# Elements 0, 1 and 31 as lists of single steps, with sums over all keys and half-size output products at the end

## The chip, the cores and the metric

The kernel runs on one core of one Trainium2 chip. The metric is device time in microseconds (us), the median of several runs. The engines that matter here are TensorE (PE: matrix products and transposes through the array), VectorE (DVE), ScalarE (ACT) and SyncE (SP, which issues nearly all transfers). Each engine works through its own queue in program order.

## The reference

32 batch elements, each with 512 nodes of 512 features (`x`) and a 512x512 adjacency (`adj`), go through two layers, all in float32. Cut to what is computed:

```python
# layer 0, H = 8 heads of 64
q, k, v = heads(x @ Wq.T + bq), heads(x @ Wk.T + bk), heads(x @ Wv.T + bv)
logits = einsum('bhqd,bhkd->bhqk', q, k) / sqrt(64)
logits = logits + log(clip(adj, 1e-8, None))[:, None]
attn = softmax(logits)                       # over the keys
out = einsum('bhqk,bhkd->bhqd', attn, v).reshape(b, n, d) @ Wo.T + bo
x = layer_norm(x + out, gamma, beta)
# layer 1, on the same adjacency
f = x @ fc_w.T + fc_b
q, k = f @ q_w.T + q_b, f @ k_w.T + k_b      # one number a node
m = leaky(q + k.T + (1 - adj) * -1e9)        # slope 0.01
y = softmax(m) @ f + x
```

## The kernel before

One element after the other. The work of neighbouring elements overlaps: while the attention of element b runs, layer 0's output product and norm and the weights of layer 1 of element b-1 (`last`) are done, and the last products of element b-2 (`gone`). Tiles hold 128 partitions; a 512x512 matrix is four tiles of 128x512. The engines' queues are filled in the order in which the Python program issues, so that order is the schedule.

Layer 0 of an element. The query, key and value products and the output product are computed by seven half-size products instead of eight (sums of quarters on VectorE, `halves` at L221, 64 columns of weights at a time, 256 wide). Heads go in four pairs. For each pair, scores are computed with the keys on the partitions (L946), ScalarE takes the exponent (L953, L955), VectorE multiplies by the clipped adjacency `cT`, turned beforehand (L963, L981: `factor`), and the value product uses the result `at` (L1049, `value_steps`). The softmax is divided out only after the value product: the sums over the keys become reciprocals `R`, spread over partitions by a round trip through DRAM (`divided`, L1114 and around), and multiply the pair's output `oT`.

These sums are taken in one of three ways. For elements 2 to 30 VectorE adds the four key tiles (L1004), turns the sum in blocks (L1008) and sums rows (L1015): "folded". For elements 0 and 1 and the first two pairs of 31, VectorE adds the four tiles to `as` (L973, L976), and `divide` multiplies that by ones on TensorE (four products a call, L1071); a ScalarE copy (L1077) and a trip through DRAM follow. For pairs 2 and 3 of 31, `divide_here` multiplies `as` by ones (L1153) and forms the reciprocal in place.

Layer 1 of an element: row dots `k` and `q` (L409), `k` spread to all partitions through DRAM (`store_k`, `load_k`: `kst`, `kld`), the mask from the adjacency (`le0`, `le1` load it), the exponent and row sums `r` (`weight_steps`), then z = weights times x with seven products (`z_steps`, sums at L1228 to L1234; the weights turned by VectorE at L636), or with whole products (`z_units`, L335) and TensorE transposes (L328), and the output product of z with `fc` (`out_steps` by seven products, or `out_units` by whole ones, L549), which VectorE adds with the residual (`yb`).

Order. Elements 2 to 30 run by two lists of single steps, `FIRST` and `SECOND`, through `perform`. In them `S0` to `S7` are score products, `f..` factors, `V..` value products, `m` products by sevens of queries and keys (`q`, `Q`), values (`v`), the output product (`w`), z (`z`) and out (`o`), `d` the differences of the next element's x, `c` the turns of the next adjacency, `la` its 16 transfers, `dv0`, `dv2` the `divided` steps, `s..` and `t..` the sums over keys. Elements 0, 1 and 31 run by functions: `slot(b, p)`, one head pair a call, with coarser units; `joining_slot(31)` and `last_slot`, `last_layer1` for the end. Before element 0 come the first transposes of x by TensorE (L656), the first queries and keys by whole products (L335) and the folding of the vectors into the weights (`fold_units`: `bias`, `offset`, `spread`).

Elements 29 and 30 differ from the others: their softmax rows are not normalised, and the factor `r` enters when the output is added (L557). Element 29's z is by sevens, element 30's by whole products with TensorE transposes; out is by whole products for both, in halves for the last. Element 31's layer 1 is by sevens throughout.

A range check (`find_range`: `over_elements`, `turn`, `over_partitions`) reduces flags on the sums to one number, `flag`; the engines load it at the end (L2009) and branch (L2011) to a general version of the kernel that the given data never need. Its last parts stand among the last products.

Of the kernel before, what the change touches and what calls it, by code (L numbers as in the profile page):

```python
# [9 lines left out]
FP = mybir.dt.float32  # L10
I32 = mybir.dt.int32
AF = mybir.ActivationFunctionType
ALU = mybir.AluOpType
# [17 lines left out]
def kernel(  # L31
# [151 lines left out]
    def combine_units(S, a11, a12, a21, a22):  # L183

        def three():
            nc.vector.tensor_add(S[:, 0], a21, a22)
            nc.vector.tensor_sub(S[:, 1], S[:, 0], a11)
            nc.vector.tensor_sub(S[:, 2], a12, S[:, 1])
        return [three, lambda: nc.vector.tensor_sub(a21, a11, a21)]
# [45 lines left out]
    def fold_units(psum, scratch):  # L235
# [15 lines left out]
        def row_times(col, w, name):  # L251

            ps = psum.tile([P, D], FP, tag="m", name=f"ps_{name}")
            for c in range(DC):
                nc.tensor.matmul(
                    ps, col[:, c : c + 1].to_broadcast([P, P]), w[:, c, :],
                    start=(c == 0), stop=(c == DC - 1),
                )
            return ps
# [6 lines left out]
        def bias():  # L266
            nc.vector.tensor_add(K["bo"], K["bo"], row_times(bvc, K["wo"], "bvwo"))
            nc.vector.tensor_sub(K["bo"][:, H:], K["bo"][:, H:], K["bo"][:, :H])
            for w, col, _, _, _, _ in vectors:
                for c in range(DC):  # L270
                    nc.vector.scalar_tensor_tensor(
                        junk, K["fc"][:, c, :], 1.0, w, ALU.mult, ALU.mult,
                        accum_out=col[:, c : c + 1],
                    )

        def offset():
            nc.vector.tensor_add(K["cc"], K["cc"], row_times(bc, K["fc"], "bfc"))
            nc.vector.tensor_add(K["cc"], K["cc"], fcb)
            nc.vector.tensor_sub(K["cc"][:, H:], K["cc"][:, H:], K["cc"][:, :H])
            for w, col, part, dg, _, b0 in vectors:  # L280
                nc.vector.tensor_mul(part, col, bc)
                nc.vector.scalar_tensor_tensor(
                    junk, fcb, 1.0, w, ALU.mult, ALU.mult, accum_out=extra[:, 1:2]
                )
                nc.vector.tensor_add(b0, b0, extra[:, 1:2])
                nc.vector.tensor_mul(col, col, gc)
                for c in range(DC):
                    nc.vector.tensor_scalar_mul(dg[:, ts(c, P)], ident, col[:, c : c + 1])
            for c in range(DC):
                nc.vector.tensor_scalar_mul(  # L290
                    K["fc"][:, c, :], K["fc"][:, c, :], gc[:, c : c + 1]
                )

        def spread(psum_parts):
            def copy(vector):
                _, _, _, dg, name, _ = vector
                ps = psum.tile([P, D], FP, tag="m", name=f"ps_{name}")
                nc.tensor.matmul(ps, ones, dg, start=True, stop=True)
                nc.vector.tensor_copy(K[name], ps)

            for vector in vectors:
                copy(vector)
            ps = psum_parts.tile([P, D], FP, tag="po", name="ps_parts")
            for i, (_, _, part, _, _, _) in enumerate(vectors):
                nc.tensor.matmul(ps[:, ts(i, DC)], ones, part, start=True, stop=True)
            for i, (_, _, _, _, _, b0) in enumerate(vectors):
                nc.vector.tensor_reduce(extra[:, 0:1], ps[:, ts(i, DC)], AX.X, ALU.add)  # L307
                nc.vector.tensor_add(b0, b0, extra[:, 0:1])

        return [bias, offset, spread]  # L310
# [163 lines left out]
    def weight_steps(s, small, name):  # L474
# [7 lines left out]
        def logit(c):  # L482
            qk = s["w"][:, (2, 3, 0)[c % 3], :]
# [83 lines left out]
    def fast(ctx):  # L567
# [9 lines left out]
        folded = {(b, p) for b in range(2, B - 1) for p in (0, 2)}  # L577
# [41 lines left out]
        def load_e(b, half=None):  # L619
# [3 lines left out]
            if b == B - 1:  # L623
                s["e"] = cT
            elif b == B - 2:
                s["e"] = K["qk_s"].rearrange("p a b f -> p (a b) f")[:, :NC, :]
            else:
                s["e"] = L1
# [19 lines left out]
        def first_xT():  # L648
# [3 lines left out]
            pt = [ps_m.tile([P, N], FP, tag="m", name=f"pt_x_{i}") for i in range(3)]  # L652
            pt.append(ps_o.tile([P, N], FP, tag="po", name="pt_x_3"))
            for c in range(NC):
                for i in range(DC):
                    nc.tensor.transpose(pt[i][:, ts(c, P)], s["n"][:, c, ts(i, P)], ident)  # L656
            for i in range(DC):
                (nc.scalar.copy, nc.vector.tensor_copy)[i % 2](s["xT"][:, i, :], pt[i])

# [12 lines left out]

        def first_qk(wq, wk):
            qk_tiles(0, 0)
            s = S[0]
            return qk_units(s, wq, wk, 0, s["qT", 0], s["kT", 0], ps_m, 0)
# [20 lines left out]

        def differences(b):
            run(difference_steps(b))
# [54 lines left out]
        def seven_qk(b, p):  # L754
            s = qk_steps(b, p)
            return [
                lambda names=names: run(s[n] for n in names.split())
                for names in ("m1 m5 cb ck2", "m6 m2 cq2 cq1", "m4 m3 ck1", "m7", "aq2 ak2 ak1")
            ]

# [38 lines left out]
        def seven_v(b):  # L799
            s = v_steps(b, long_banks(b))  # L800
            return [
                lambda names=names: run(s[n] for n in names.split())
                for names in ("m1 m5 cb c22", "m6 m2 c12 c11", "m7 m3 a22 a12", "m4 c21")
            ]

# [34 lines left out]
        def wo_steps(b, banks, apart=False):  # L840
# [9 lines left out]
            if apart:  # L850
                data["21"] = [third[:, c, :] for c in range(KH)]
# [16 lines left out]
            steps = row_steps(data, sub, K["wo_s"], K["wo"], lambda n: ps[n], add, apart)  # L868
            return steps | {"seed": seed}

        def seven_wo(b, banks, apart=False):
            s = wo_steps(b, banks, apart)

            def unit(names):
                return lambda: run(s[n] for n in names.split())
            adds = [[s[n] for n in names.split()] for names in (
                "s11 a11", "s12 a01 a00", "b11 b01", "a10 b10" if apart else "a10")]
            return [s["seed"]] + [
                unit(names) for names in ("m1 m5 cb", "m2 m6", "m3 m7", "m4")
            ], adds  # L880
# [77 lines left out]
        def factors(b, p, half):  # L958

            s = S[b]  # L960
            for kc in (2 * half, 2 * half + 1):
                at = s["at", p, kc]
                nc.vector.scalar_tensor_tensor(  # L963
                    at, cT[:, kc, :].unsqueeze(1).to_broadcast([P, 2, N]), ADJ_MIN, at,
                    ALU.max, ALU.mult,
                )

        def sums(b, p, half):

            s = S[b]  # L970
            if half == 0:
                s["as", p] = act.tile([P, 2, N], FP, tag="at", name=f"as_{b}_{p}", bufs=8)
                nc.vector.tensor_add(s["as", p], s["at", p, 0], s["at", p, 1])  # L973
            else:
                for kc in (2, 3):
                    nc.vector.tensor_add(s["as", p], s["as", p], s["at", p, kc])  # L976

# [7 lines left out]

        def both(b, p):
            run(values(b, p))

        def sums_in_place(b, p):

            s = S[b]
            to = s["as", p] = s["at", p, 0]
            return [
                lambda kc=kc: nc.vector.tensor_add(to, to, s["at", p, kc]) for kc in range(1, NC)
            ]
# [65 lines left out]
        def values(b, p):  # L1061
            v = value_steps(b, p)
            return [v["a"], lambda: (v["b"](), v["e"]())]

        def divide(b, p):


            s = S[b]
            ps = lone[0]
            for h in range(4):  # L1070
                nc.tensor.matmul(  # L1071
                    ps[h * BL : (h + 1) * BL, :], ones[:, :BL], s["as", p + h // 2][:, h % 2, :],
                    start=True, stop=True,
                )
            s["R", p] = act.tile([P, 2, N], FP, tag="R", name=f"R_{b}_{p}")
            r = s["R", p][:, 0, :]
            nc.scalar.copy(r, ps)  # L1077
            m = 4 * N // P
            d0 = dram.tile([4, N], FP, tag="d0", name=f"d0_{b}_{p}")
            nc.sync.dma_start(out=d0, in_=r.rearrange("(h r) n -> h r n", r=BL)[:, 0, :])  # L1080
            c = small.tile([P, 2, m], FP, tag="c", name=f"c_{b}_{p}", bufs=2)
            nc.sync.dma_start(out=c[:, 0, :], in_=d0.rearrange("h (a m) -> (h a) m", m=m))
            s["c", p] = c
# [974 lines left out]
```

## Time and profile before

| | us |
|---|---|
| median of 3 runs | 3292.02 (3288.52 to 3293.7) |
| profiled execution | 3290.96 |
| its span | 3289.1 |
| TensorE, VectorE, ScalarE busy | 3265.4, 3075.6, 1461.7 |
| granted TensorE clock | 0.998 |

The span runs from the first to the last record of the profiled execution. The times of the engines' rows overlap a little with the next row's, since operations are pipelined: from start to start a 64-column, 256-wide product unit takes 0.2156 us (two records), a 128-column, 512-wide one 0.86, a 64-column, 512-wide one 0.43. In the profile L12 means line 12 of the kernel, an arrow names what is written and read, and a wait says what the waiting engine waited for and how long in all, how often, and the longest.

### The profile page before, as it was taken

Reading aid. Unit: us, or ns where it says so; the run is one execution under the profiler, and the core shown is the slowest. Engines: PE = TensorE matmul, PEld = TensorE weight load, DVE = VectorE, ACT = ScalarE, POOL = GpSimd, SP = SyncE. Lnnn points to the kernel's source line nnn. Section 1 sums busy time; section 2 is a strip of 40 time slices with the busy share of each in tenths; the row PEclk is TensorE's granted clock in tenths of the full one; section 3 lists DMA queues with packets and bytes.
Section 4 is the critical chain, followed back from the end, with each engine's and each line's share of the span. In section 5 each row is a group of like instructions: output and inputs, shape, how many; then the busy total and the mean of one; then the engine's idle time right before and its main releaser. Section 6 shows DMA issues by size and latency. Waiting matters only on the chain.

```text
span 3289.1 us, 63772 instructions
## 1 busy us (share of the span) xinstructions
PE 3265.4 (99%) x25450; PEld 1885.3 (57%) x25450; DVE 3075.6 (94%) x5319; ACT 1461.7 (44%) x2733; POOL 1.0 (0%) x10
## 2 busy tenths in 40 slices
PE   9999999999999999999999999999999999999999
PEld 4555555555555555555556555555555555555545
DVE  7889999999999999999999999999999999999998
ACT  3435434444444354344444443543445444445432
POOL 0000000000000000000000000000000000000000
PEclk9999999999999999999999999999999999999999
DMA  5243433443433434334434334343343333442421
GB/s 129 42 79 70 89 75 65 85 90 70 86 69 71 95 70 88 71 65 89 88 71 84 68 73 95 68 89 72 61 95 84 75 82 66 76 96 64 95 70 43
DMA packets 914598, 256.14 MB, mean 78 GB/s; under 512 B 839908, under 2 KB 842212, under 8 KB 914296
## 3 DMA queue, kind: packets, MB, share of 16 engines
q1 hardware_dynamic: 914296, 252.01, 38.0%
q8 instruction: 202, 3.31, 0.5%
q14 instruction: 100, 0.82, 0.1%
HBM read 183.88 MB, written 36.55 MB: 67 GB/s over the span
## 4 chain that ended last, share of the span: by engine, by line
PE 97%; DVE 2%; ACT 1%; DMA 0%; issue 0%; SPq 0%; DVEq 0%; ACTq 0%
PE f L221 23%; PE mx L221 15%; PE my L221 15%; PE mz L221 15%; PE po L1049 13%; PE sc L946 7%; PE my L946 2%; PE mx L946 2%; PE mz L946 2%; DVE at L963 0%; PE my L335 0%; PE mz L549 0%; ACT n L399 0%; DMA n<-in_x_dram 0%; DVE R L409 0%
## 5 line engine op out<-in xcount | busy, mean ns | idle before, releaser
L981 DVE SCALAR_TENSOR_TENSOR at<-cT,at 128x1024 f32<-128x1024 f32 x468 | 557.1, 1211 | 1.8 <-ACT at L953 1.8
L1049 PE MATMUL po<-at,v 128*64 128x512 f32 x2048 | 486.5, 596 | 1.3 <-DVE fold_more L307 0.9
L726 ACT ACTIVATE qT<-f,bq 128x256 f32<-128x256 f32 x254 | 115.3, 470 | 805.0 <-PE f L221 805.0
L1004 DVE TENSOR_TENSOR at<-at,at 128x1024 f32<-128x1024 f32 x348 | 418.2, 1209 | 0.0
L955 ACT ACTIVATE at<-sc 128x1024 f32<-128x1024 f32 x270 | 272.7, 1072 | 48.1 <-PE sc L946 48.1
L1049 PEld LDWEIGHTS po<-at,v 128*64 128x64 f32 x2048 | 140.4, 137 | 230.2 <-issue 138.9
L221 PE MATMUL f<-xT,wq 128*64 128x256 f32 x2032 | 262.5, 379 | 0.0
L946 PE MATMUL sc<-qT,kT 64*128 64x512 f32 x1080 | 256.9, 592 | 0.3 <-ACT at L955 0.3
L221 PE MATMUL f<-T,qk_s 128*64 128x256 f32 x2032 | 256.4, 379 | 0.1
L221 PEld LDWEIGHTS f<-xT,wq 128*64 128x64 f32 x2032 | 146.3, 137 | 100.3 <-issue 36.0
L221 PEld LDWEIGHTS f<-T,qk_s 128*64 128x64 f32 x2032 | 146.1, 137 | 85.9 <-issue 16.6
L946 PEld LDWEIGHTS sc<-qT,kT 64*128 64x128 f32 x1080 | 103.7, 187 | 131.1 <-issue 87.2
L726 ACT ACTIVATE kT<-f,bk 128x256 f32<-128x256 f32 x254 | 120.0, 472 | 120.7 <-PE f L221 119.2
L1008 DVE STREAM_TRANSPOSE at<-at 128x1024 f32<-128x1024 f32 x116 | 142.3, 1227 | 1.0
L1015 DVE TENSOR_REDUCE ks<-at 128x32 f32<-128x1024 f32 x116 | 139.6, 1204 | 1.0
L221 PE MATMUL f<-xT,qk_s 128*64 128x256 f32 x1016 | 131.2, 379 | 0.0
L221 PE MATMUL f<-T,wk 128*64 128x256 f32 x1016 | 131.2, 379 | 0.0
L221 PE MATMUL f<-xT,wk 128*64 128x256 f32 x1016 | 131.2, 379 | 0.0
L946 PE MATMUL mz<-qT,kT 64*128 64x512 f32 x252 | 130.5, 598 | 0.0
L946 PE MATMUL my<-qT,kT 64*128 64x512 f32 x246 | 127.1, 597 | 0.0
L946 PE MATMUL mx<-qT,kT 64*128 64x512 f32 x238 | 123.4, 598 | 1.7 <-ACT R L1077 1.7
L946 PE MATMUL so<-qT,kT 64*128 64x512 f32 x232 | 124.1, 615 | 0.0
(431 smaller groups left out, 6446.5 us busy)
## 6 DMA issues: line engine op xcount, KB each, us to landing
cT<-in_adj_dram SPq DMA_DIRECT2D x512, 64.0 KB
R<-d SPq DMA_DIRECT2D x126, 256.0 KB
x<-in_x_dram SPq DMA_DIRECT2D x124, 256.0 KB
n<-in_x_dram SPq DMA_DIRECT2D x31, 1024.0 KB
L<-in_adj_dram SPq DMA_DIRECT2D x60, 512.0 KB
eP<-L SPq DMA_DIRECT2D x480, 64.0 KB
out_dram<-yb SPq DMA_DIRECT2D x58, 512.0 KB
w<-dk SPq DMA_DIRECT2D x32, 256.0 KB
```

The costliest lines, as they stand in the source:

```text
L221: nc.tensor.matmul(to[ts(h, DK)], left[:, ts(h, DK)], right, start=start, stop=stop, skip_group_check=True,)
L726: nc.scalar.activation(of(w, half), ps[bank], AF.Identity, bias=bias)
L946: nc.tensor.matmul(parts[j], s["kT", p][rows, ts(kc, P)], s["qT", p][rows, :], start=True, stop=True,)
L955: nc.scalar.activation(at, sc, AF.Exp, scale=SCALE)
L981: nc.vector.scalar_tensor_tensor(at, cT[:, kc, :].unsqueeze(1).to_broadcast([P, 2, N]), ADJ_MIN, at, ALU.max, ALU.mult,)
L1004: nc.vector.tensor_add(to, to, s["at", p, kc])
L1008: nc.vector.transpose(flat, flat)
L1015: nc.vector.tensor_reduce(ks.rearrange("p h m -> p (h m)"), flat.rearrange("p (a k) -> p a k", k=BL), AX.X, ALU.add,)
L1049: nc.tensor.matmul(s["po", p][j * DK : (j + 1) * DK, :], s["v"][h // 4][:, kc, ts(h % 4, DK)], s["at", p, kc][:, j, :], start=(kc == 0), s ...
```

## The change

- Elements 0, 1 and 31 get lists of single steps of their own, `FIRST0`, `SECOND0`, `FIRST1`, `SECOND1`, `FIRST_LAST`, `SECOND_LAST`, and run through `first_two` and `second_two` like the others. `slot`, `joining_slot`, `last_slot` and the coarse units go. The folding of the weights is cut into single steps (`B`, `D`, `O`, `P`, `G`) that stand in the lists.
- The key sums of elements 0 and 1 and of the first two pairs of 31 are the folded ones; `sums` and `divide` go. For pairs 2 and 3 of 31 `divide_here` multiplies the four key tiles by ones, without adding them first.
- The softmax rows of elements 29, 30 and 31 are normalised as those of the others. Out of elements 29 and 30 is by seven products. Element 30 keeps whole products for z and TensorE transposes (steps `Z` and `J`), element 31's layer 1 keeps its sevens (steps `L`), with a changed order of the last products and the accumulators of out started from the constant row `cc`.
- The range check comes after the last addition (`rg0 rg1 Lot2 rg2`).

The core of the diff:

```diff
-        def divide(b, p):
-            s = S[b]
-            ps = lone[0]
-            for h in range(4):
-                nc.tensor.matmul(
-                    ps[h * BL : (h + 1) * BL, :], ones[:, :BL], s["as", p + h // 2][:, h % 2, :],
-                    start=True, stop=True,
-                )
...
         def divided(b, p):
...
-            if (b, p) in folded:
-                c = small.tile([P, 2, m], FP, tag="c", name=f"c_{b}_{p}", bufs=2)
-                nc.vector.tensor_reduce(
-                    c[:, 0, :], s["c4", p].rearrange("p k m -> p m k"), AX.X, ALU.add
-                )
-            else:
-                c = s["c", p]
+            c = small.tile([P, 2, m], FP, tag="c", name=f"c_{b}_{p}", bufs=2)
+            nc.vector.tensor_reduce(
+                c[:, 0, :], s["c4", p].rearrange("p k m -> p m k"), AX.X, ALU.add
+            )
...
-            def add():
-                for j in range(2):
-                    nc.tensor.matmul(
-                        ps[j * DK : (j + 1) * DK, :], ones[:, :DK], s["as", p][:, j, :],
-                        start=True, stop=True,
-                    )
+            def add(half):
+                if half == 0:
+                    x["ps"] = ps_s.tile([P, 2, N], FP, tag="s", name=f"ps_{b}_{p}")[:, 0, :]
+                for kc in (2 * half, 2 * half + 1):
+                    for j in range(2):
+                        nc.tensor.matmul(
+                            x["ps"][j * DK : (j + 1) * DK, :], ones[:, :DK],
+                            s["at", p, kc][:, j, :], start=(kc == 0), stop=(kc == NC - 1),
+                        )
...
+        SECOND1 = """
+            x0 n0 le1 S0 S1 n2 S2 x2 x1 n4 t10 le0 S3 k1 t11 S4 mv0 S5 mk0 d0 n1 S6
...
+            V3b qaq2 lg3 lk2 qm4 lk0 nm lk3 s20 ex2 va12 ex3 Qm1 qck1 R3 vm2 la R2
+            ex0 ex1 inv s21 c0 s30 Qcb nr1 nr0 va22 nr3 vc11 s22 V3e Qm5 s31 nr2 Qm6
...
+        SECOND_LAST = """
+            t10 n0 zd S0 S1 S2 S3 S4 S5 f20 f23 f21 S6 oseed t11 S7 f22 f31 V2a om1
+            n1 zs f30 mv0 ldn H20 n2 V2b n4 k1 n3 k0 k3 k2 os11 H30 u0 ocb om2 k4 u2
...
+            Loa10 Loa01 Loa11 Lom7 Loa000 Lot3 Lob10 Lot4 Lob11 Lot0 Lot1 Lom3 Lob01
+            rg0 rg1 Lot2 rg2
+        """
...
+        special = {0: (FIRST0, SECOND0), 1: (FIRST1, SECOND1), B - 1: (FIRST_LAST, SECOND_LAST)}
         for b in range(B):
-            if 2 <= b < B - 1:
-                first_two(b)
-                second_two(b)
-                continue
-            if b == B - 1:
-                joining_slot(b)
-            for p in range(b == B - 1, NPAIR):
-                if b == B - 1 and p == 3:
-                    flag = last_slot(rest)
-                else:
-                    rest = slot(b, p)
-        return flag
+            orders = special.get(b, (FIRST, SECOND))
+            first_two(b, orders[0])
+            second_two(b, orders[1])
+        return S[B - 1]["flag"]
```

In the lists of element 31, `H20` to `H34` are the steps of `divide_here` for pairs 2 and 3, `W..` the output product of its layer 0, `O..` and `Y..` out and its sums for element 30, and `L..` the last products (`Lm` z, `Lom` out, `Lob`, `Loa` additions, `Lot` stores); `x..` are its layer 1 weights (`xkst`, `xkld` the rows of `k`).

## The prediction

> **What bounds the kernel now.** I read the page's busy shares and its chain first.
>
> ```profile
> PE 3265.4 (99%) x25450; PEld 1885.3 (57%) x25450; DVE 3075.6 (94%) x5319; ACT 1461.7 (44%) x2733; POOL 1.0 (0%) x10
> PE 97%; DVE 2%; ACT 1%; DMA 0%; issue 0%; SPq 0%; DVEq 0%; ACTq 0%
> ```
>
> TensorE is the chain, so on average only less TensorE work can help. An average over 3289 us says little of the two ends, which are all that changes here. So next the windows (columns: window, length, then busy us of PE, PEld, DVE, ACT, POOL, granted clock, DMA share, GB/s).
>
> ```profile
> 0.00:100.00 100.00, 95.82 (x622) 52.87 (x624) 73.85 (x122) 35.75 (x58) 1.00 (x10) 1.00 0.51 122
> 100.00:200.00 100.00, 93.69 (x678) 50.00 (x676) 81.66 (x149) 45.58 (x83) 0.00 (x0) 0.98 0.35 57
> 300.00:400.00 100.00, 100.00 (x798) 58.25 (x796) 95.15 (x164) 45.21 (x86) 0.00 (x0) 1.00 0.39 78
> 3100.00:3200.00 100.00, 95.02 (x640) 49.84 (x638) 90.90 (x154) 37.78 (x69) 0.00 (x0) 0.97 0.32 80
> 3200.00:3289.00 89.00, 80.97 (x478) 43.21 (x474) 74.34 (x156) 28.91 (x57) 0.00 (x0) 0.98 0.16 52
> ```
>
> In the middle TensorE never stops, and VectorE is close behind (95%). It stops only in the first 200 us (elements 0 and 1) and the last 170 (element 31). TensorE's waits name the stops:
>
> ```profile
> PE my L221 <- DVE eP L636: 4.7, 1, 4.7
> PE mx L221 <- DVE v L781: 2.8, 1, 2.8
> PE mx L946 <- ACT R L1077: 1.7, 1, 1.7
> PE po L1049 <- DVE fold_more L307: 0.9, 1, 0.9
> PE my L221 <- DVE T L689: 0.8, 1, 0.8
> ```
>
> TensorE's timeline then shows what a stop costs beyond itself (start, length, group; the wait in brackets):
>
> ```profile
> 183.97 3.38 PE L221 MATMUL mx<-wv,T 128*64 128x256 f32 x16 [2.78 <-DVE v L781]
> 187.19 3.60 PE L1049 MATMUL po<-at,v 128*64 128x512 f32 x16
> 3129.20 3.62 PE L221 MATMUL my<-eP,n 128*64 128x256 f32 x16 [4.72 <-DVE eP L636]
> 3132.65 1.68 PE L221 MATMUL mz<-R,third 128*64 128x256 f32 x14
> ```
>
> Such a group of 16 otherwise takes 1.90 us. After 2.78 and 4.72 us of idleness it took 3.38 and 3.62, so these two stops cost about 1.5 and 1.7 more; after the stops of 0.8, 0.9 and 1.7 no group was long.
>
> **The middle.** Element 2's first score starts at 199.56, element 31's at 3119.87: 29 periods of 100.70 us. The program's TensorE order between element 3's first score and element 31's is the same 4900 rows in both kernels, waits included; VectorE and ScalarE gain there only the normalising of element 29's rows (one reciprocal, four scalings). So I cost the middle at nothing: ScalarE, 45% busy, hides the scalings. Without that cover they cost 4 x 0.5 us.
>
> **The head, to element 2's first score, 199.56 now.** Removed: four `divide` groups of products with ones (L1071). One starts at 104.27 and the next group at 105.26: 4 x 0.99 = 4.0. If the new lists close the waits `v` (2.8 and its 1.5 of long group), `R` (1.7), `fold_more` (0.9) and `T` (0.8), that is 7.7. The `R` wait is `divide` itself: its ScalarE copy held one of the three shared banks. Together 11.7, a first score at 187.9.
>
> Against that stands VectorE. The old sums are three additions of 128x1024 a pair and the new ones add turns and row sums (`L1008` 1227 ns, `L1015` 1204 ns, each four times an element), of which the last few fall behind element 2's first score, as in the middle. Adding VectorE's program in order, with rows' start-to-start times (1.13 us for a 1024-wide operation, 0.61 for 512, 0.34 for 256), gives 152 us to element 2's first score before and 163 after; busy were 155.5. Of the 163, 81 belong to element 1, where TensorE's summed work is 77.7, some 80 with changes of group. So in element 1 both are full, and VectorE will be late in places. Walking both queues side by side I find: the seventh value product of element 0 behind `d3`, which stands behind a turn of the adjacency whose transfer lands late (1.2); the scores behind pair 1's queries and keys (0.6 and 0.5); value products V0 and V2 behind factors (0.7 and 1.2); the last value product of element 1 behind its subtraction (1.7). That is 5.9 if all add up, 3.6 if the late VectorE is caught up during the other stops. I take 4.2, nearer to the second since VectorE works on while TensorE waits elsewhere. First score at 187.9 + 4.2 = 192.1: **gain 7.5**, bounds 4 and 11. Each new stop is under 1.8 us, in the row's range without a long group.
>
> The Trainium skill, TensorE: Matmul & The Clock Gate, Part 1, has the array fall to half clock after an idle window of about 3.4 us. The row disagrees: 2.78 us was enough. By the page the 1.5 us would not belong to that stop, and the head's gain would be 6.0; the sum stays with the row.
>
> **The tail, 3119.87 to 3289.1 now.** TensorE's last product ends 163.3 us after element 31's first score, the last addition at 3283.68, the span 5.4 later.
> - Order. The four turns of `eP` (L636, 2.48 us at 3127.85) now come under pair 2's query products instead of behind element 31's scores: the 4.72 wait and its 1.7 go, 6.4.
> - `divide_here` (L1153, 64x512, some 0.43 us a product) multiplies all four key tiles rather than a sum: 4 products become 16, +5.2. VectorE loses the additions, but TensorE is what is full here. `divide` for pair 0 goes, -1.0.
> - The last two elements' output products become seven half-size ones: 28 whole 128x512 at 0.86 and 8 of 0.43 are 27.5; 112 units of 0.2156 are 24.2: -3.3. Their additions, about 0.34 us per 128x256 part, lie under products.
> - Whole products and turns for element 30 stay as many as before.
>
> Net work +0.9. Smaller stops (0.3 to 0.7, six, 2.3 in all) go or are replaced: `Lm1` behind the copies of turned weights (0.7), `Lm7` behind the copy out of its bank (0.65), the first turn of element 30's weights behind their scaling (0 to 1.2, I take 0.6). Last product: 163.3 - 6.4 + 0.9 - 2.3 + 1.9 = 157.4, 5.9 earlier; walking both queues side by side gives 155.8, 7.5 earlier. I take the middle, **6.7**.
>
> The last chain: the range check. Now its flag is ready at 3279.9, ahead of the last additions; after the change six small VectorE operations, two turns and two reductions follow the last addition.
>
> ```profile
> L2011 PEldq COMPARE_BRANCH  x1: 4475/4475/4475, 3281.4 to 3281.4; - x1
> L2011 DVEq COMPARE_BRANCH  x1: 76/76/76, 3284.1 to 3284.1; - x1
> L2011 DVEq EVENT_SEMAPHORE  x1: 21/21/21, 3287.3 to 3287.3; - x1
> ```
>
> VectorE's branch already followed its last addition, and it took 3.1 us to its next instruction. The check adds about ten operations of 0.15 to 0.2 and two hand-overs of 0.3: 2.3, less 0.2 of overlap, so **2.1 lost** (0 to 2.6).
>
> Weight folds cut into single steps add no instruction. `la`, the 16 transfers of the next adjacency, keeps its place behind the last factor `f33`; SP is also moved past `dv0`'s store and spread, both issued before `f33` ends. The rows `kst` to `kld` of element 31 take 6.4 us in the trace of before and now lie under the whole products (13.8 us): nothing, or up to 6.4 if `k` comes behind them.
>
> **Sum.** The profiled execution took 3290.96, 1.9 more than its span of 3289.1 and 1.1 less than the median of 3292.02. 3290.96 - 7.5 - 6.7 + 2.1 = 3278.9; I say **3279**. What can be told from no change is 0.2%, 6.6 us: below 3285.4 is faster.
>
> The change leans on 64-column products. The Trainium skill, same page, Part 3, says "If K<128 or M<128, most of the 128×128 array sits idle". By that, 112 half-width units would cost as much as 128-column ones, 0.43 instead of 0.2156, and the time would be 24 later, 3303. The trace refutes it: half the columns take half as long (L221 0.107 us per record, L549 at the same 256 width 0.223).
>
> **Rivals.**
> - *VectorE paces the head* (0.13). For it: 81 us in element 1 against 77.7, and lists that were never timed against transfers. Against: in the middle it holds 95% without stopping TensorE. At its present share of the second window, 81.66%, 163 us take 200, and with the 5 before its first operation the first score is at 205; the tail's 4.6 remains: 3291.8. The head's gain is gone at a share of 84%: 3286.4; the forecast needs 87%.
> - *A late adjacency, slower* (0.06). `la` waits for `f33`, and its first turn `c0` stands in element 1's list only some 7 us of VectorE's work behind `f33`. Sixteen issues of 0.53 us and 2 us of landing are 10.5; the first quarter needs 4.1, so it fits with 2.9 to spare. If SP is held by `dv0`'s round trip for longer, the turns, the factors and the scores behind them wait. A whole load exposed in elements 0 and 1, each with 1.5 of long group, is 24: 3303. It decides once a load is exposed by more than 7.8 us in each, which with the long groups adds 18.6.
> - *Only the tail's end goes wrong* (0.05): `J` and `kld` late (1.2 + 6.4) with the flag's 2.6, 7.5 more than I took: 3286.5, no change.
> - *The change does not act as written* (0.01): if the middle shifted phase by 0.5 us a period, 14.5 us would be lost, 3293.5.
>
> **Numbers.** The forecast, both ends shorter, has 0.75: 3279, its own bounds 3271.8 (head 11.7, tail 7.5, check 0) and 3285.1 (head 4, tail 4.5, check 2.6). The rivals reach beyond; leaving out about a tenth at each end, and with the runs' own scatter of some 2 us below, gives 3270 to 3289. Faster by over 0.2%: the 0.75 and a third of the VectorE rival's spread, 0.79; within: the rest of it, the tail's and the last rival, 0.14; slower: 0.07.
>
> **What would show it.** Element 2's first score near 192 and element 31's 2920 after it; no TensorE wait on `eP` and none on `R` before element 2; VectorE over 85% in the second window; last product 156 to 157 after element 31's first score, the span 7 to 8 after the last addition. A stop over 2.7 us in either end, a period other than 100.7, or VectorE under 82% in the head would prove me wrong.

## The result and the profile after

| | before | after |
|---|---|---|
| median of 22 runs, us | 3291.34 (3288.4 to 3293.7) | 3286.53 (3281.79 to 3289.14) |
| profiled execution, us | 3290.96 | 3286.61 |
| its span | 3289.1 | 3282.6 |
| time outside the span | 1.9 | 4.0 |
| start to element 2's first score | 199.56 | 198.83 |
| from there to element 31's first score | 2920.31 | 2920.99 |
| from there to the last addition | 163.81 | 155.19 |
| from there to the end of the span | 5.4 | 7.6 |

The ratio is 0.9986 (95% interval 0.9979 to 0.9992): 4.8 us or 0.14% faster. That is inside the stated range (3270 to 3289), but of the 12 us that were forecast less than half came, and by the 0.2% bound it counts as no change, which had a chance of 0.14; the case that had 0.79, faster by over 0.2%, did not come.

The table says where it went. The tail (from element 31's first score to the last addition) gained 8.6, more than forecast; the check at the end took 2.2 back, as forecast. The head, forecast at 7.5, gained 0.7; the middle lost the same; and 2.1 us appeared outside the span, where nothing was forecast.

The page's busy shares and chain, and the windows (the same columns as before):

```profile
PE 3258.3 (99%) x25586; PEld 1890.9 (58%) x25586; DVE 3080.4 (94%) x5329; ACT 1471.5 (45%) x2762; POOL 1.0 (0%) x10
PE 97%; SPq 1%; ACT 1%; DVE 1%; DMA 0%; issue 0%; DVEq 0%; ACTq 0%
```

```profile
0.00:100.00 100.00, 91.07 (x564) 48.81 (x566) 70.02 (x102) 33.46 (x59) 1.01 (x10) 0.98 0.52 119
100.00:200.00 100.00, 95.78 (x710) 52.89 (x708) 95.31 (x181) 45.04 (x88) 0.00 (x0) 0.98 0.34 55
300.00:400.00 100.00, 100.00 (x794) 58.00 (x792) 95.00 (x165) 45.36 (x86) 0.00 (x0) 1.00 0.41 78
3100.00:3200.00 100.00, 100.00 (x738) 56.49 (x736) 93.64 (x165) 44.64 (x84) 0.00 (x0) 1.00 0.28 68
```

The window from 3100 to 3200 is now full (95.02 before). The first window is emptier than before (91.07 for 95.82), and in the second VectorE is at 95%, its share in the middle. TensorE's waits, in the same form as before:

```profile
PE mx L221 <- DVE xT L695: 3.5, 1, 3.5
PE my L221 <- ACT at L926: 2.2, 1, 2.2
PE pf L1162 <- DVE low L1158: 1.9, 1, 1.9
PE pw_a L221 <- DVE oT L846: 1.2, 1, 1.2
PE f L221 <- ACT qT L723: 1.0, 1, 1.0
PE f L221 <- ACT kT L723: 0.9, 1, 0.9
```

All five stops shown of before are gone: `eP`, `v`, `R`, `fold_more` and `T`. But the head has two new ones of the same size, `xT` and the exponent L926, and both have a group at half speed behind them as well (its products start twice as far apart). TensorE's timeline:

```profile
25.71 3.63 PE L221 MATMUL mx<-wv,xT 128*64 128x256 f32 x16 [3.48 <-DVE xT L695]
33.47 0.69 PE L919 MATMUL mx<-qT,kT 64*128 64x512 f32 x1 [0.68 <-ACT v L786]
...
162.08 3.50 PE L221 MATMUL my<-wv,xT 128*64 128x256 f32 x16 [2.17 <-ACT at L926]
```

The first stop is 3.48 and 1.73 (3.63 for 1.90), the second 2.17 and 1.6. With 0.68, 0.49, 0.53, 0.11, 1.00 and 0.93 that is 12.7 us of stops and half speed in the head. Without them element 2's first score would stand at 186.1, so the prediction's floor of 187.9 was near; its 4.2 us of new stops was not.

VectorE's timeline shows what the first stop hangs on:

```profile
17.90 1.23 DVE L185 TENSOR_TENSOR qk_s<-wk 128x1024 f32<-128x1024 f32 x1 [4.05 <-DMA wk<-in_wkT_dram]
...
22.53 1.18 DVE L188 TENSOR_TENSOR wk<-wq,wk 128x1024 f32<-128x1024 f32 x1
24.28 0.71 DVE L667 STREAM_TRANSPOSE cT<-cT 128x512 f32<-128x512 f32 x1 [0.57 <-DMA cT<-in_adj_dram]
24.91 0.65 DVE L695 TENSOR_TENSOR xT<-xT 128x512 f32<-128x512 f32 x1
```

The difference `d3` (L695), which TensorE waits for, stands behind `c2`, the turn of a part of the adjacency, and behind a series of sums for the weights that had itself waited 4.05 us for the key weights. Its own inputs were there nearly ten microseconds earlier: TensorE's last reading of the whole x ends at 15.17.

How long this stop lasts differs from execution to execution, and only one of each kernel is traced. With the same steps in front of it the wait on `xT` was 3.48 here, 2.64 in e5, 2.42 in e3, 2.38 in e2, 1.92 in e6 and 1.29 in e10. Element 2's first score stood at 198.83 here, and at 197.77 (e3), 196.95 (e6) and 195.67 (e10) in the runs below that leave the head's lists as they are (e10 only adds small transposes while TensorE waits). So the 0.7 that the head gained here, against the 199.56 of before, is the least of four readings, 0.7 to 3.9.

### The profile page after: what moved, and what is told of

Its sections match the earlier page's. It is cut to its first block, busy times and chain, and to the rows that moved or that the text cites. A ratio compares the mean times of both kernels' runs of the same rounds, so it can differ in the third digit from the quotient of the medians.

```text
span 3282.6 us, 64089 instructions
## 1 busy us (share of the span) xinstructions
PE 3258.3 (99%) x25586; PEld 1890.9 (58%) x25586; DVE 3080.4 (94%) x5329; ACT 1471.5 (45%) x2762; POOL 1.0 (0%) x10
## 4 chain that ended last, share of the span: by engine, by line
PE 97%; SPq 1%; ACT 1%; DVE 1%; DMA 0%; issue 0%; DVEq 0%; ACTq 0%
PE f L221 23%; PE my L221 15%; PE mz L221 15%; PE mx L221 15%; PE po L991 13%; PE sc L919 6%; PE mx L919 2%; PE my L919 2%; PE mz L919 2%; SPq L604 0%; SPq L150 0%; PE mx L334 0%; ACT at L926 0%; PE ps L1056 0%; ACT at L928 0%
## 5 line engine op out<-in xcount | busy, mean ns | idle before, releaser
L934 DVE SCALAR_TENSOR_TENSOR at<-cT,at 128x1024 f32<-128x1024 f32 x512 | 608.7, 1210 | 3.3 <-ACT at L928 3.3
L723 ACT ACTIVATE qT<-f,bq 128x256 f32<-128x256 f32 x254 | 115.8, 471 | 805.0 <-PE f L221 805.0
L946 DVE TENSOR_TENSOR at<-at,at 128x1024 f32<-128x1024 f32 x378 | 454.5, 1209 | 2.4 <-PE po L991 2.1
L928 ACT ACTIVATE at<-sc 128x1024 f32<-128x1024 f32 x256 | 259.1, 1073 | 5.0 <-DVE ks L957 2.5
L919 PE MATMUL sc<-qT,kT 64*128 64x512 f32 x1024 | 241.9, 589 | 0.0
L723 ACT ACTIVATE kT<-f,bk 128x256 f32<-128x256 f32 x254 | 120.1, 473 | 136.9 <-PE f L221 128.8
L950 DVE STREAM_TRANSPOSE at<-at 128x1024 f32<-128x1024 f32 x126 | 154.5, 1226 | 1.1
L957 DVE TENSOR_REDUCE ks<-at 128x32 f32<-128x1024 f32 x126 | 151.5, 1203 | 1.0
L919 PE MATMUL so<-qT,kT 64*128 64x512 f32 x256 | 137.1, 615 | 0.0
L919 PE MATMUL mx<-qT,kT 64*128 64x512 f32 x256 | 132.7, 598 | 1.2 <-ACT v L786 0.7
```

The lines of the kernel that those rows point to most:

```text
L723: nc.scalar.activation(of(w, half), ps[bank], AF.Identity, bias=bias)
L919: nc.tensor.matmul(parts[j], s["kT", p][rows, ts(kc, P)], s["qT", p][rows, :], start=True, stop=True,)
L928: nc.scalar.activation(at, sc, AF.Exp, scale=SCALE)
L934: nc.vector.scalar_tensor_tensor(at, cT[:, kc, :].unsqueeze(1).to_broadcast([P, 2, N]), ADJ_MIN, at, ALU.max, ALU.mult,)
L950: nc.vector.transpose(flat, flat)
L957: nc.vector.tensor_reduce(ks.rearrange("p h m -> p (h m)"), flat.rearrange("p (a k) -> p a k", k=BL), AX.X, ALU.add,)
```

## Experiments

The theory after the result: the head's stops are places in the lists, where an engine's queue is held by something that the waiting step does not need. The rival is the one of the prediction: VectorE, full in element 1, paces the head whatever the order.

Distances to the changed kernel are between medians of different rounds. The kernel before stood at 3291.34, 3291.16, 3291.72 and 3290.90 in these rounds, so a distance of less than a microsecond says nothing.

**Two differences ahead of the weights' sums (e1).**

```diff
-            ... A1 g1 h0 h1 h2 g4 vm1 vcb vm5 vm6
-            c0 h3 c2 vc12 vm2 d3 vm7 vc22 g2 d2 va22 vc11 c1
+            ... A1 g1 d3 d2 g2 h0 h1 h2 g4 vm1 vcb vm5 vm6
+            c0 h3 c2 vc12 vm2 vm7 vc22 va22 vc11 c1
```

> In the changed kernel TensorE stands 3.48 us before element 0's seventh value product (22.23 to 25.71) and the group after it takes 3.63 us instead of 1.90. Here the two differences d3 and d2 and the sum g2 stand before h0, where VectorE waits 4.05 us for the key weights, so nothing behind them waits for the adjacency. My theory (the stop is an order error, not a lack of VectorE time): the stop goes, element 0's first score at 28.2 instead of 33.5, and 4 to 5.2 us of it last to element 2's first score (194 instead of 198.8); time 3282 for 3286.5. Rival (VectorE paces elements 0 and 1, so a freed stop comes back later): first score at 28.2, but element 2's at 197.5 or later, time within 1.3 us of the changed kernel.

Measured: 3283.58, ratio to before 0.9977 (0.9967 to 0.9987), 3.0 below the changed kernel. The wait on `xT` is gone and element 0's first score stands at 27.88. Element 2's stands at 196.47, 2.4 earlier and not 4 to 5. The rest came back at element 0's next scores, where 0.53 became 2.07 with half speed behind it (scores of 0.59 took 1.06):

```profile
40.46 1.01 PE L919 MATMUL mx<-qT,kT 64*128 64x512 f32 x1 [2.07 <-DVE kT L727]
41.26 1.06 PE L919 MATMUL mx<-qT,kT 64*128 64x512 f32 x1
```

Neither expectation is met in full. The queue was freed, but the next late transfer in it, the row of q_w that step `D0` waits for, was the new end.

**The value product behind the scores (e2).**

```diff
-            ... S2 x2 x1 n4 t10 le0 S3 k1 t11 S4 mv0 S5 mk0 d0 n1 S6
-            vm1 k3 n3 x3 S7 k0 qm1
+            ... S2 x2 x1 t10 le0 S3 k1 t11 S4 mv0 S5 n4 mk0 d0 S6 n1 S7
+            vm1 k3 n3 x3 k0 qm1
```

> In the changed kernel TensorE stands 2.18 us before element 1's vm1 (159.91 to 162.08), whose bank ScalarE reads last, behind two normalisations n2 and n4 of 0.84 each; the group after it takes 3.50 us. Here vm1 stands behind the scores S7, n4 behind S5 and n1 behind S6. Theory (the order of the list, through ScalarE's queue): the stop falls below 0.6, no long group, 3 to 3.4 us gained at element 2's first score (195.5), time 3283. Rival (VectorE or the score banks pace this place): S7 or the first query product waits instead, gain under 1 us.

Measured: 3286.48, ratio 0.9985 (0.9976 to 0.9994), no different from the changed kernel. The 2.17 fell to 0.60 and no long group followed, yet element 1 lasted 85.96 for 86.06: the wait on a key copy (L723) grew from 0.9 to 2.0, and new ones on other copies came (0.6 and 0.3). Nothing was gained, as the rival had it; but most of the new waits are on ScalarE's copies, so this run does not show that VectorE is the reason.

**The check ahead of the end (e3).** `rg0` behind `Wb01`, `rg1` behind `J3`, `rg2` behind `Z0`, after the last sums that they read.

> The range check (rg0, rg1, rg2) is moved from behind the last addition to the products of element 31's layer 0 and the first whole product of z, after the last sum that it reads. Theory 1: the check at the end costs 2.1 us inside the span (the end of the span 5.4 after the last addition instead of 7.55) and is also why the time lies 3.5 to 4.0 above the span instead of 1.9: time 4 lower, 3282.5. Theory 2: the part outside the span comes from something else (the longer program or its start): the span falls by 2.1, the time by 2.1, and the part outside stays at 3.4 to 4.0.

Measured: 3282.35, ratio 0.9976 (0.9966 to 0.9986), 4.2 below the changed kernel; the part outside the span fell from 3.65 (median) to 2.02. In size theory 1 is right. That the check's place is the cause of the outside part did not survive e9 and e10 below.

**VectorE relieved (e5).** The turns (L950) of elements 0 and 1 are left out, and a small memset stands for each row sum.

> Leaves out the turns and row sums of the key sums of elements 0 and 1 (constant sums in their place, so those two elements are not divided by their softmax sums): 16 VectorE operations of 1.15 us start to start, some 18 us of VectorE's work in the first 200 us, of which 13 before element 2's first score. Rival (VectorE full in element 1, as the prediction had it): the stops after 155 us shrink, element 2's first score 4 us or more earlier, time 3282 or less. Theory (the stops are list order and ScalarE's queue): TensorE's waits on xT (3.5) and on the score's exponent (2.2) stay as they are, element 2's first score moves by less than 1.5 us, time within 1.5 of the changed kernel.

Measured: 3284.52, ratio 0.9979 (0.997 to 0.9988), 2.0 below the changed kernel. The waits on `xT` (2.6 in this run) and on the exponent (2.17) stay, as the theory had it. In the traces element 1 is 85.06 instead of 86.06, and element 2 is 100.69 instead of 101.52. Only the second of these belongs to VectorE. Element 1 also lasts 85.05 in e6 and 85.04 in e10, where VectorE has all its work, and 86.06 in e1, e3 and e7. What differs is the clock behind the stop of 2.17: from 100 to 200 us it is 0.98 in the changed kernel, e1, e3 and e7, and 1.00 here, in e6 and in e10. In e10 the group behind the stop took 1.95 us, in the changed kernel 3.50:

```profile
159.93 1.95 PE L221 MATMUL my<-wv,xT 128*64 128x256 f32 x16 [2.16 <-ACT at L929]
```

So the traces put VectorE's new work at 0.8 us, a backlog that is paid in element 2, and nothing in element 1. How much of the 2.0 between the medians is the clock is not known. By the same measure e2, at a clock of 1.00, is 0.9 longer in element 1 than e6 and e10. VectorE's load is a cost, but not the larger one.

**The sums of pairs 2 and 3 undone (e6).**

```diff
+                to = s["at", p, 0]
...
+                for kc in (2, 3):
+                    nc.vector.tensor_add(to, to, s["at", p, kc])
...
-                            s["at", p, kc][:, j, :], start=(kc == 0), stop=(kc == NC - 1),
+                        to[:, j, :], start=True, stop=True,
```

> Undoes one part: for pairs 2 and 3 of element 31 VectorE adds the four key tiles in place (three additions of 128x1024 a pair, 6.8 us start to start) and TensorE multiplies the sum by ones, 4 products of 64x512 instead of 16. The prediction's term (TensorE is what is full at the end): TensorE's work falls by 5.2, the last addition comes 4 to 5 us earlier, time 3282. Rival (VectorE, 94% busy there, is late with the sums, so the products over all keys are worth their price): the waits behind VectorE in 3180 to 3215 grow by as much or more, time 3286 to 3290.

Measured: 3296.14, ratio 1.0015 (1.0006 to 1.0024), 9.6 above the changed kernel. The span alone is some 11 us longer (median), since the part outside it is 1.82 here. The rival is right, and the loss is even larger than it expected. TensorE's waits in this stretch:

```profile
PE ps L1060 <- DVE at L1057: 9.1, 2, 5.7
PE mz L221 <- DVE yb L871: 2.6, 1, 2.6
```

12 products of 0.43 are saved and 11.7 us of waiting come in their place, with half speed behind it. The prediction counted those 5.2 as a plain cost; here they buy more than they cost. Beside the lines shown, the edit moves one step (`H30`, pair 3's first addition) behind the first value product of pair 3 (`V3a`); otherwise the lists are not rearranged for the additions. So 9.6 is what this order costs, and a better one may cost less.

**Element 0 mended, and the check early (e7).** e1 and e3, and in `FIRST0`:

```diff
-            ... pm1 pcb D0 pm5 pm6 ... f02 D1 D2 pm4 pm3 pck1
-            pm7 paq2 pak1 D3 S4 S5 pak2 S6 f12
+            ... pm1 pcb pm5 pm6 ... f02 pm4 pm3 pck1
+            pm7 paq2 pak1 S4 S5 pak2 S6 D0 D1 D2 D3 f12
```

> The early d3, d2, g2 of e1 and the early check of e3, and D0 to D3 (which wait on VectorE's queue for the rows of q_w, and with them the queries and keys of pair 1 behind them) moved behind S6. In e1 the freed stop came back in part at S4: 2.07 us instead of 0.53, with a group at half speed after it. Theory (VectorE's queue held by a late transfer, not VectorE's work): S4's wait falls to 0.6, element 2's first score near 193 instead of 196.5, time 3283.6 - 4 - 3 = 3277. Rival (element 1 absorbs it: what element 0 gains is given back before element 2): element 2's first score at 196, time 3280.

Measured: 3278.09, ratio 0.9961 (0.9947 to 0.9974), 8.4 below the changed kernel. It is the fastest kernel here that does the whole computation. Against e3, which differs from it only in element 0's list, it is 4.3 lower. Element 2's first score stands at 193.80 and S4's wait at 0.53, as the theory asked. The waits in the head are then what element 1 leaves:

```profile
PE my L221 <- ACT at L926: 2.2, 1, 2.2
PE f L221 <- ACT qT L723: 1.0, 1, 1.0
PE f L221 <- ACT kT L723: 0.9, 1, 0.9
```

**Element 1 as well (e8).** e7 with e2, and the row scalings `nr0` to `nr3` moved behind the copies of queries and keys.

> e7 with vm1 behind S7 (e2) and the four row scalings nr of element 0 moved behind the query and key copies that they stood before in ScalarE's queue (in e2 the wait on such a copy grew from 0.9 to 2.0 and took back what vm1 gave). Theory (in element 1 it is ScalarE's queue): S0 of element 1 to S0 of element 2 falls from 86.0 to 83.5 or less, time 2.5 below e7. Rival (VectorE's work paces element 1 whatever the order, 81 us of it): it stays at 85.5 to 86, time within 1 of e7.

Measured: 3278.37, ratio 0.9961 (0.9947 to 0.9974), the same as e7. Element 1 did shrink, to 83.77: 2.3 below e7, of which 1.0 is the half-speed group that this trace does not have. Element 2 grew from 101.53 to 103.56:

```profile
195.66 1.99 PE L919 MATMUL sc<-qT,kT 64*128 64x512 f32 x8 [1.75 <-DVE kT L727]
```

The scores of element 2 wait for VectorE, which is late with the last key additions. What the order gave, VectorE's backlog took back in element 2. The theory was right that this order shortens element 1, and the rival about the time.

**Both limits off (e11).** e8 with the turns and row sums left out as in e5.

> e8 with the turns and row sums of elements 0 and 1 left out as in e5 (those two elements not divided by their sums). e8 shortened element 1 by 2.3 us on TensorE and gave 2.0 back in element 2; e5 alone took 18 us off VectorE for 2.0. Theory (two limits lie on each other: the order in ScalarE's queue, and behind it VectorE's backlog): together they give more than either, element 1 at 83 or less and element 2's period at 100.7, time 3278.4 - 3.5 = 3275 or less. Rival (the gains just add, or VectorE's backlog is not what e8 met): time 3276.5 to 3278.

Measured: 3276.5, ratio 0.9954 (0.994 to 0.9967), 1.9 below e8. Element 1 stays at 83.76, element 2 falls to 101.7. By the times the gains add (2.0 in e5, 1.9 here, but only 1.0 when e8 and e11 are each set against the kernel before in their own round), as the rival had it. The traces speak in part for the theory: without the turns element 2 is 0.8 shorter with the changed kernel's order (e5) and 1.85 shorter with e8's. Which of the two holds stays open. What is left of the head's stops in this run (1.00 in element 1, 0.74 at element 2's scores, and eight of 0.3 to 0.7) was not taken apart.

**The check last in the kernel before (e9).** Only the three calls of the check moved behind the last addition.

> The kernel before, with only its range check moved behind the last addition. Theory (a check at the end costs inside the span and as much again outside it): the time lies 3.4 to 4 above the span instead of 1.9, the last addition to the span's end 7.5 instead of 5.4, time 3295 for 3291.2. Rival (what the changed kernel adds outside its span belongs to its other parts): the part outside stays 1.9, time 3293.

Measured: 3294.26, ratio 1.0008 (0.9999 to 1.0017), 2.5 above the kernel before in the same runs (3291.72). The interval just reaches 1, but the trace agrees: from the last addition to the span's end it takes 7.84 for 5.38. The part outside the span is 1.82, as the rival had it. So a check at the end costs its 2 to 2.5 us inside the span, and nothing outside by itself.

**TensorE's stream shifted (e10).** 24 transposes of 2x2 ahead of the first transposes of x, where TensorE waits anyway.

> The changed kernel with 24 transposes of 2x2 put on TensorE while it waits for the first part of x (3.7 us), so that every later instruction of TensorE lies 24 pairs further on. The part of the time outside the span was 3.2 to 4.1 in the changed kernel, e1, e2 and e5, and 1.7 to 2.1 in the kernel before, e3, e6, e7, e8 and e9; e6 and e9 have the check last as well. Theory (where the last instructions come to lie in TensorE's stream matters; e6 has 24 products less): the part outside falls to 1.8 to 2.1, time 3285. Rival (something else): it stays at 3.2 to 4, time 3286.5.

Measured: 3285.51, ratio 0.9981 (0.9972 to 0.999). The part outside the span is 1.78 to 1.91 in all 11 runs, for 3.17 to 4.09 in the changed kernel. The time is only 1.0 below the changed kernel: the spans of these runs were 0.7 longer in the median, and single runs scatter over 7 us. These 24 pairs take the increase of the outside part away, and that part of the theory is shown. That it is the place of TensorE's last instructions that counts is not shown: no row is recorded there, so what the pairs avoid, and whether at the start or at the end, stays open.

## Why the prediction was right, and where it was not

The time lies inside the range, but the head's gain of 0.7 lies outside the head's own bounds (4 to 11). The forecast's own bounds ended at 3285.1; the range holds because it was widened for the rivals, and because the tail gained more than was summed; that the two errors partly cancel is luck. Of the signs that were named ahead, the tail's end and VectorE's share in the second window (95.31%) came, and no wait on `eP` or `R` was left; a stop over 2.7 us (3.48) and a period other than 100.7 (101.52, element 2) came as well, and they were to prove the forecast wrong.

**The middle at nothing.** Nearly: 2920.99 for 2920.31. Element 2 alone is longer, 101.52 for 100.69, and the later periods are the same within 0.2. The 0.7 is VectorE's backlog from element 1, since it goes with the turns (in e5 element 2 takes 100.69 again). The prediction compared the program, which is the same, and not the state in which the engines enter it.

**The head's work.** Right within 2 us: floor 186.1 for 187.9. The removed stops all went, and VectorE's work up to element 2's first score is 164 us for the 163 that were summed.

**The head's new stops.** This step failed: 12.7 for 4.2 (7.8 in e10, the shortest of the traces with this head). It failed in three ways.
- The stop behind `d3` was named, but sized 1.2; it was 3.48, and 1.29 to 2.64 in the other traces. Its cause was named in part: the adjacency's 16 issues took 17.6 us on SP, one alone 3.47, but VectorE stood only 0.57 us for the adjacency and 4.05 for the key weights ahead of it. e1 and e7 show that the whole stop was a matter of place.
- The stops charged to VectorE in element 1 (V0 and V2 behind factors, 1.9; the last value product, 1.7) did not occur. In their place came four at ScalarE's results, 2.17, 1.00, 0.93 and 0.11, that the prediction did not have. It added up VectorE's queue and took ScalarE, 45% busy, for cover; but ahead of and behind the exponent that frees the bank stand ten other exponents and four normalisations, and from 154.8 to 164.3 that queue does not pause.
- Both long stops brought a group at half speed, 3.3 together. The prediction expected none, because no single stop was to be over 1.8. Of the second group's 1.6 a part comes back: the later wait on the key copy is 0.93 behind it and 1.57 without it (e10), so element 1 is longer by 1.0.

The rival of VectorE pacing the head came nearest to the outcome in the head (its gain gone), but not for its reason: with 18 us less of VectorE's work 2 us came back by the medians, of which the traces give VectorE 0.8 (e5), and with the order of element 0 mended 5 did (e7 against the changed kernel at element 2's first score; 4.3 against e3 by the medians). What paces element 1 is not settled: e2 and e8 took its longest stop away and did not gain time.

**The tail.** Right in mechanism and a little small: last product 154.45 after element 31's first score (up to 155.4 in e10), where the terms gave 157.4 and the walk 155.8. The `eP` stop is gone with its half-speed group. The three stops forecast there are 0.46 for 0.7 (`Lm1`), 0.69 for 0.65 (`Lm7`) and 0.2 for 0.6 (the first turns); one of 1.22 (`pw_a` behind an output) was not seen coming.

**The end.** 2.2 for 2.1, and 2.5 when tried alone (e9). The branch rows, TensorE's first:

```profile
L1749 PEldq COMPARE_BRANCH  x1: 3558/3558/3558, 3278.0 to 3278.0; - x1
L1749 DVEq EVENT_SEMAPHORE  x1: 21/21/21, 3280.9 to 3280.9; - x1
```

TensorE's branch takes 3.6 us here and took 4.5 before; VectorE's next instruction comes 2.9 us after its branch at 3278.0, for 3.1 before.

**Outside the span.** The sum carried 1.9 over from before; it is 3.17 to 4.09, median 3.65. No row shows it. e10 shows that 24 more pairs of instructions on TensorE take the increase away; the mechanism stays open.

**The late adjacency, the slower rival.** `la` in element 1 did not come late. The adjacency that did come late was element 0's, and VectorE stood 0.57 us for it; the whole stop behind that queue, with its long group, cost 5.2, not 24.

With the head's 6.7 (8.5 more of stops, a floor 1.8 lower), the middle's 0.7, the outside part's 2.1 and 0.3 at the end, less the 2.1 by which the last product came earlier than forecast, 3278.9 becomes 3286.6; the profiled execution took 3286.61. e7 then reached 3278.1 by mending two places in element 0's list and the check's.

## What to carry to other kernels

When a hand order is made finer, the sum of each engine's work tells the floor, and the stops are decided by what stands in front of a needed step in its own queue: look above all for a step that waits for a transfer and is not needed soon, and put it behind. Walk the queue of the engine that is half idle too, since a burst on it stops the full engine as well as any shortage. A stop mended on one engine is a gain only if the next engine has slack at that place: in element 0 it had, and in element 1 it was given back in the next element. Before two traces of one stretch are set against each other, compare the clock in it: a microsecond of element 1 went with the clock and not with the edit.

## What the runs showed of the hardware

- The half-speed group does not come after a fixed length of idleness. The same stop of 2.17 us in front of the same group of 16 products was followed by 3.50 us for the group in the changed kernel, 3.28 in e1, 3.13 in e3, 2.69 in e7, and by the plain 1.95 in e5, e6 and e10; after 2.4 us in e2 and e3 (the `xT` stop) the group took 1.95. Whenever it came behind the stop of 2.17, it cost the same: from the start of the group to the first query product behind the four scores it took 4.58 us in all four traces, and 2.93 or 2.94 in the three without it. In e7 the first products behind the stop are 0.21 us apart, as at full speed, and from the middle of the group 0.41. The Trainium skill, TensorE: Matmul & The Clock Gate, Part 1, calls the window of activity free-running, not tied to the kernel; that agrees with this scatter. Its length of about 3.4 us of idleness does not: 2.07 us was enough in e1.
- The start of an execution varies by some 3 us: the first value product starts between 14.42 (e1) and 17.48 (e6) with the same transfers ahead of it. TensorE's waits on the parts of x differ by 0.9 of that (3.59 and 4.51); the rest was not taken apart.
- Up to 2.2 us more of a run's time than usual (4.09 for 1.9) can lie outside the recorded rows, and 24 pairs of instructions more on TensorE took them away in all 11 runs. A change of a few microseconds should be read from the time and the span together.
